# A Mamba scan moved to (channel, state) partitions: one-hot products on TensorE, the C product on GpSimd, convolution and projections folded into TensorE

## The chip, the cores and the metric

One core of one Trainium2 chip. The metric is the device time of one execution in microseconds (us). Fast executions of one kernel agree within 1% here (the widest apart are 10080.98 and 10161.75 us), and only executions of the fast state are compared. A ratio is the mean time of one kernel's fast runs over the mean time of the fast runs of the kernel before in the same rounds, so it is not quite the ratio of the medians that are quoted.

## The reference, cut to what matters

A non-local attention, a convolution block with a Mamba layer ("layer 1"), a bidirectional Mamba along both image axes ("layer 2", four more sets of weights), and a dynamic filter. The part that changes is the Mamba layer, which runs five times:

```
xz = einsum('blc,dc->bld', h, in_proj_w);  xm, z = split(xz, 2)
xc = silu(conv1d(xm, convd_w, causal, depthwise, 4 taps) + convd_b)
dt, B, C = split(einsum('bld,ed->ble', xc, x_proj_w), [4, 16, 16])
dt = softplus(einsum('blr,dr->bld', dt, dt_proj_w) + dt_proj_b)
step:  h = exp(dt*A) * h + dt*B*xc;   y = einsum('bds,bs->bd', h, C)     # 128 channels d, 16 states s
y = (y + xc*Dp) * silu(z);  return einsum('bld,cd->blc', y, out_proj_w)
```

All data are float32.

## The kernel before

128 channels lie on the partitions. A unit of the scan is 768 tokens of one batch and direction; it takes sixteen steps, one for each state. B and C of a state are one value a token, and TensorE copies them to all partitions with a broadcast product; the sum over states is an identity product that accumulates in PSUM.

```
for s in range(D_STATE):                              # one step = one state, 128 channels x 768 tokens
    nc.scalar.activation(da, u.dt, AF.Exp, scale=w.A[:, s : s + 1])
    ...                                               # zero da where a sequence starts
    if last is not None: add(*last)                   # y += identity x hc: two products
    cs = self.broadcast(w.C[s], u.xc)                 # two products of 384 columns
    nc.vector.tensor_mul(two(bx), two(u.u), bs)       # u * B
    if s + 1 < D_STATE: bs = self.broadcast(w.B[s + 1], u.xc)      # two products
    nc.vector.tensor_tensor_scan(h, da, bx, init, ALU.mult, ALU.add)
    nc.vector.tensor_mul(two(hc), two(h), cs)         # h * C
    next(other, None)                                 # a piece of the next unit's head
```

The head of the next unit (projection, convolution with four VectorE instructions, gate, step width dt by softplus, u = dt * xc) is a generator of which one piece is taken a step.

Of the kernel before, what the change touches and what calls it, by code (L numbers as in the profile page):

```python
# [26 lines left out]
P = 128  # L27
# [41 lines left out]
def rows_of(b):  # L69
    return slice(b * C, (b + 1) * C)  # L70

# [344 lines left out]
def mamba_weights(k, pool, i):  # L416

    nc = k.nc
    a = pool.tile([P, D_STATE], FP, name=f"A{i}")
    nc.scalar.activation(a, k.col(f"A_log{i}"), AF.Exp)  # L420
    nc.vector.tensor_scalar_mul(a, a, -1.0)
    in_w = k.mat(f"in_w{i}")
    if i:
        nc.vector.tensor_scalar_mul(in_w, in_w, k.col(f"norm_w{i}"))
    x_w = k.mat(f"x_w{i}")
    return SimpleNamespace(
        A=a,
        in_w=in_w,
        dt_x=x_w[:, :DT_RANK],
        B=[x_w[:, DT_RANK + s : DT_RANK + s + 1].to_broadcast([P, P]) for s in range(D_STATE)],  # L430
        C=[x_w[:, DT_RANK + D_STATE + s : DT_RANK + D_STATE + s + 1].to_broadcast([P, P]) for s in range(D_STATE)],
        dt_w=k.dtw[:, bass.ts(i, P)],
        conv_w=k.col(f"convd_w{i}"),
        conv_b=k.col(f"convd_b{i}"),
        dt_b=k.col(f"dt_b{i}"),
        Dp=k.col(f"Dp{i}"),
        out_w=k.mat(f"out_w{i}"),
    )


class Mamba:
# [8 lines left out]
    def __init__(self, k, wk, ps_bc, ps_y, ps_m):  # L450
        self.k, self.nc = k, k.nc
        self.wk, self.ps_bc, self.ps_y, self.ps_m = wk, ps_bc, ps_y, ps_m

    def mm(self, lhsT, rhs, m=P):
        p = self.ps_m.tile([P, NB], FP, tag="m", name="mm")
        self.nc.tensor.matmul(p[:m, :HALF], lhsT=lhsT, rhs=rhs, start=True, stop=True)  # L456
        return p[:m, :HALF]

    def work(self, tag, **kw):
        return self.wk.tile([P, CH], FP, tag=tag, name=tag, **kw)  # L460

    def head(self, u):
# [3 lines left out]
        tokens = [self.k.xb[rows, u.c0 + j * HALF : u.c0 + (j + 1) * HALF] for j in range(2)]  # L466
        pad = D_CONV - 1

        n, t = (1, CH) if u.carry else (SEQS, W)
        xp = self.wk.tile([P, n * (t + pad)], FP, tag="xp", name="xp")  # L470
        xp3 = xp.rearrange("p (n t) -> p n t", n=n)
        at = 0 if u.rev else pad
        edge = xp3[:, :, t:] if u.rev else xp3[:, :, :pad]
        if u.carry:
            nc.gpsimd.tensor_copy(edge[:, 0, :], u.carry.hist)
        else:
            nc.gpsimd.memset(edge, 0.0)
        for j in range(2):
            p = self.mm(w.in_w[rows, :P], tokens[j])
            if u.carry:  # L480
                nc.scalar.copy(xp[:, at + j * HALF : at + (j + 1) * HALF], p)
            else:
                m = SEQS // 2
                nc.scalar.copy(xp3[:, j * m : (j + 1) * m, at : at + W], p.rearrange("p (n t) -> p n t", n=m))  # L484
        if u.carry:
            nc.gpsimd.tensor_copy(u.carry.hist, xp[:, CH:])
        yield

        acc = self.work("acc", bufs=1)
        acc3 = acc.rearrange("p (n t) -> p n t", n=n)  # L490
        for j in range(D_CONV):
            by = j if u.rev else pad - j
            tap = w.conv_w[:, pad - j : pad - j + 1]
            if j == 0:
                nc.vector.tensor_scalar(acc3, xp3[:, :, by : by + t], tap, w.conv_b, ALU.mult, ALU.add)
            else:
                nc.vector.scalar_tensor_tensor(acc3, xp3[:, :, by : by + t], tap, acc3, ALU.mult, ALU.add)  # L497
                yield

        u.xc, u.gate = self.work("xc"), self.work("gate")  # L500
        pz = [self.mm(w.in_w[rows, P:], tokens[j]) for j in range(2)]
        nc.scalar.activation(u.xc, acc, AF.Silu)
        for j in range(2):
            nc.scalar.activation(u.gate[:, halves[j]], pz[j], AF.Silu)  # L504
# [4 lines left out]
        low = self.wk.tile([DT_RANK, CH], FP, tag="low", name="low", bufs=1)  # L509
        for j in range(2):  # L510
            nc.scalar.copy(low[:, halves[j]], self.mm(w.dt_x, u.xc[:, halves[j]], DT_RANK))
        yield
        e, u.dt = self.work("e", bufs=1), self.work("dt")
        for j in range(2):
            p = self.mm(w.dt_w, low[:, halves[j]])
            nc.scalar.activation(e[:, halves[j]], p, AF.Abs, bias=w.dt_b)
            nc.scalar.activation(u.dt[:, halves[j]], p, AF.Relu, bias=w.dt_b)
        yield
# [3 lines left out]
        yield  # L522
# [3 lines left out]
        nc.gpsimd.tensor_add(log, log, e)  # L526
        nc.gpsimd.tensor_add(u.dt, u.dt, log)
        yield
        u.u = self.work("u")
        nc.gpsimd.tensor_mul(u.u, u.dt, u.xc)  # L530

    def broadcast(self, lhsT, xc):

        p = self.ps_bc.tile([P, 2, NB], FP, tag="bc", name="bc")
        for j in range(2):
            self.nc.tensor.matmul(p[:, j, :HALF], lhsT=lhsT, rhs=xc[:, bass.ts(j, HALF)], start=True, stop=True)  # L536
        return p[:, :, :HALF]

    def scan(self, u, other):
        nc, w = self.nc, u.w  # L540
        y = self.ps_y.tile([P, 2, NB], FP, tag="y", name="y_ssm")

        def two(t):
            return t.rearrange("p (j n) -> p j n", j=2)

        def add(s, hc):
            for j in range(2):
                nc.tensor.matmul(  # L548
                    y[:, j, :HALF], lhsT=self.k.ident, rhs=hc[:, bass.ts(j, HALF)], start=s == 0, stop=s == D_STATE - 1
                )  # L550

        bs = self.broadcast(w.B[0], u.xc)
        last = None
        for s in range(D_STATE):
            da = self.work("da", bufs=3)
            nc.scalar.activation(da, u.dt, AF.Exp, scale=w.A[:, s : s + 1])  # L556
            if not u.carry:

                first = W - 1 if u.rev else 0
                nc.gpsimd.memset(da.rearrange("p (n t) -> p n t", n=SEQS)[:, :, first : first + 1], 0.0)  # L560
            if last is not None:
                add(*last)
            cs = self.broadcast(w.C[s], u.xc)
            bx = self.work("bx")
            nc.vector.tensor_mul(two(bx), two(u.u), bs)  # L565
            if s + 1 < D_STATE:
                bs = self.broadcast(w.B[s + 1], u.xc)
            h = self.work("h")
            step = slice(None, None, -1) if u.rev else slice(None)
            init = u.carry.state[:, s : s + 1] if u.carry else 0.0  # L570
            nc.vector.tensor_tensor_scan(h[:, step], da[:, step], bx[:, step], init, ALU.mult, ALU.add)  # L571
            if u.carry:
                nc.gpsimd.tensor_copy(u.carry.state[:, s : s + 1], h[:, CH - 1 :])
            hc = self.work("hc", bufs=3)
            nc.vector.tensor_mul(two(hc), two(h), cs)  # L575
            last = s, hc
            next(other, None)
        add(*last)
        yv = self.work("yv", bufs=1)
        nc.vector.scalar_tensor_tensor(two(yv), two(u.xc), w.Dp, y[:, :, :HALF], ALU.mult, ALU.add)  # L580
        u.y = self.work("yg", bufs=3)
        nc.gpsimd.tensor_mul(u.y, yv, u.gate)

    def run(self, units):

        for _ in self.head(units[0]):
            pass
        for i, u in enumerate(units):
            before = units[i - 1].tail(units[i - 1]) if i else ()
            after = self.head(units[i + 1]) if i + 1 < len(units) else ()  # L590
            other = chain(before, after)
            self.scan(u, other)
            for _ in other:
                pass
        for _ in units[-1].tail(units[-1]):
            pass


def mamba_pools(tc):
# [3 lines left out]
        tc.tile_pool(name="ssm_bc", bufs=2, space=PSUM),  # L603
        tc.tile_pool(name="ssm_y", bufs=1, space=PSUM),
        tc.tile_pool(name="ssm_m", bufs=2, space=PSUM),
# [3 lines left out]
def layer1(k):  # L609
# [41 lines left out]
    with ExitStack() as pools:  # L651
        ws, *rest = [pools.enter_context(p) for p in mamba_pools(tc)]
        m = Mamba(k, *rest)
        w = mamba_weights(k, ws, 0)
        carries = []
        for b in range(B):
            hist = ws.tile([P, D_CONV - 1], FP, name=f"hist{b}")
            state = ws.tile([P, D_STATE], FP, name=f"state{b}")
            nc.gpsimd.memset(hist, 0.0)
            nc.gpsimd.memset(state, 0.0)  # L660
            carries.append(SimpleNamespace(hist=hist, state=state))
# [25 lines left out]
def bi_mamba(k, which, along_h, lin_w, lin_b):  # L687
# [27 lines left out]
    with ExitStack() as pools:  # L715
        ws, *rest = [pools.enter_context(p) for p in mamba_pools(tc)]
        m = Mamba(k, *rest)
        w = [mamba_weights(k, ws, i) for i in which]
# [4 lines left out]
        def tail(u):  # L723
            rows = rows_of(u.b)
            n = HALF // W
            for j in range(2):
                s0 = u.c0 // W + j * n
                x = xs[rows, s0 : s0 + n, :]
                p = m.ps_m.tile([P, NB], FP, tag="m", name="po_bi")
                for d, one in enumerate((u.forward, u)):  # L730
                    at = rows_of(d)
                    nc.tensor.matmul(  # L732
                        p[at, :HALF], lhsT=w[d].out_w, rhs=one.y[:, bass.ts(j, HALF)], start=True, stop=False
                    )
                    nc.tensor.matmul(  # L735
# [160 lines left out]
```

## Time and profile before

| what | before |
|---|---|
| time | 12640.72 us (12632.42 to 12644.66) |
| scan stages, 120 units | 9350 us, 78 us a unit |
| all else (attention, norms, filter) | 3284 us |
| TensorE busy | 94% |
| VectorE busy | 79% |
| GpSimd busy | 14% |
| granted TensorE clock, mean | 0.977 |

TensorE is the bound and two engines have room. The lines that show it are in the prediction; read the busy shares first, then the wait behind each VectorE group: VectorE waits for broadcast products (953 us in all), TensorE waits for little (29 us before its broadcast products, 319 before its identity products).

### The profile page before, as it was taken

What the parts mean: (1) busy time and instruction counts of PE and PEld (TensorE: products, weight loads), DVE (VectorE), ACT (ScalarE), POOL (GpSimd) and SP (SyncE); (2) the same over time, 40 slices, a digit from 0 to 9 for tenths busy, and PEclk for the clock granted to TensorE, in tenths of its full rate; (3) what the DMA queues carried; (4) which work ended last, traced back from release to release, by engine and by line L of the source; (5) the groups of instructions that cost most, each with busy time, mean ns of one, the idle gap of its engine ahead of it and who ended that gap; (6) DMA issues with size and microseconds to landing.
All of it is one profiled execution on the core that took longest, in us unless ns stands there. A gap on an engine that the chain in (4) does not pass through costs nothing. (4 is left out here: it accounts for less than half of the span.)

```text
span 12634.1 us, 96887 instructions
## 1 busy us (share of the span) xinstructions
PE 11881.0 (94%) x37382; PEld 5579.8 (44%) x37382; DVE 10031.1 (79%) x7909; ACT 4985.3 (39%) x5408; POOL 1789.1 (14%) x2732
## 2 busy tenths in 40 slices
PE   9999999987999998999999999998999999999996
PEld 3333333323444443444444444443444444444443
DVE  4666566667888888888888888887888888888888
ACT  3444344444333333333333333333333333333332
POOL 0000000002222221111111111110111111111110
PEclk9999899998999998999999999998999999999998
DMA  0000000000000000000000000000000000000000
GB/s 20 1 1 1 1 1 1 1 1 0 0 0 0 0 0 0 0 0 1 0 0 0 0 0 1 0 0 0 0 0 1 0 0 0 0 0 0 0 0 15
DMA packets 2206, 17.03 MB, mean 1 GB/s; under 512 B 196, under 2 KB 324, under 8 KB 1096
## 3 DMA queue, kind: packets, MB, share of 16 engines
q1 hardware_dynamic: 1440, 9.44, 0.2%
q8 instruction: 294, 4.82, 0.2%
q14 instruction: 176, 1.44, 0.0%
q10 hardware_dynamic: 296, 1.33, 0.0%
HBM read 6.05 MB, written 4.72 MB: 1 GB/s over the span
## 5 line engine op out<-in xcount | busy, mean ns | idle before, releaser
L536 PE MATMUL bc<-xc,mats 128*128 128x384 f32 x15360 | 5282.9, 487 | 29.2 <-DVE bx L565 29.2
L536 PEld LDWEIGHTS bc<-xc,mats 128*128 128x128 f32 x15360 | 2924.9, 190 | 2077.4 <-DVE bx L565 34.4
L556 ACT ACTIVATE da<-dt,A 128x768 f32<-128x768 f32 x1920 | 1798.1, 937 | 4300.6 <-DVE h L571 4029.6
L548 PE MATMUL y_ssm<-hc,ident 128*128 128x384 f32 x7680 | 2963.8, 509 | 319.2 <-DVE hc L575 296.6
L571 DVE TENSOR_TENSOR_SCAN h<-da,bx 128x768 f32<-128x768 f32 x1536 | 2939.5, 1914 | 143.3 <-DVE bx L565 3.2
L575 DVE TENSOR_TENSOR hc<-h,bc 128x768 f32<-128x768 f32 x1920 | 1831.3, 954 | 752.3 <-PE bc L536 639.0
L548 PEld LDWEIGHTS y_ssm<-hc,ident 128*128 128x128 f32 x7680 | 1304.3, 189 | 1902.7 <-DVE hc L575 990.4
L565 DVE TENSOR_TENSOR bx<-u,bc 128x768 f32<-128x768 f32 x1920 | 1828.6, 952 | 326.6 <-PE bc L536 314.3
L267 DVE TENSOR_TENSOR acc_e<-acc_e,e 128x1536 f32<-128x1536 f32 x792 | 1390.3, 1755 | 763.2 <-ACT e L211 724.5
L211 ACT ACTIVATE e<-f_exp 128x1536 f32<-128x1536 f32 x864 | 1207.2, 1449 | 1218.9 <-PE f_exp L201 1218.9
L218 PE MATMUL y_att<-e,xb 128*64 128x512 f32 x5184 | 1242.5, 601 | 0.0
L201 PE MATMUL f_exp<-theta,phi 64*128 64x512 f32 x5184 | 1236.4, 608 | 0.4 <-ACT e L211 0.4
L560 POOL MEMSET da<- 128x8 f32 x1536 | 166.2, 113 | 5575.7 <-ACT da L556 5575.7
L201 PEld LDWEIGHTS f_exp<-theta,phi 64*128 64x128 f32 x5184 | 469.1, 187 | 757.0 <-issue 463.7
L571 DVE TENSOR_TENSOR_SCAN h<-da,state,bx 128x768 f32<-128x768 f32 x384 | 763.7, 1989 | 42.1 <-DVE bx L565 0.5
L218 PEld LDWEIGHTS y_att<-e,xb 128*64 128x64 f32 x5184 | 341.3, 136 | 830.7 <-issue 830.1
L556 ACT ACT_TABLE_LOAD x351 | 450.3, 1283 | 65.6 <-DVE h L571 60.6
L456 PE MATMUL mm<-xb,mats 64*128 64x384 f32 x960 | 422.9, 534 | 38.5 <-ACT xp L484 15.4
L240 POOL TENSOR_TENSOR xa<-xa,t_att 64x512 f32<-64x512 f32 x36 | 45.4, 1261 | 2721.6 <-ACT t_att L238 2721.6
L525 POOL TENSOR_TENSOR e<-e,kept 128x768 f32<-128x768 f32 x120 | 360.9, 3008 | 313.8 <-ACT log L521 313.8
L497 DVE SCALAR_TENSOR_TENSOR acc<-xp,cols,acc 128x768 f32<-128x768 f32 x360 | 374.1, 1039 | 7.4
L504 ACT ACT_TABLE_LOAD x234 | 300.2, 1283 | 151.8 <-PE mm L456 148.9
(124 smaller groups left out, 5499.1 us busy)
## 6 DMA issues: line engine op xcount, KB each, us to landing
xa<-in_x SPq DMA_DIRECT2D x6, 768.0 KB, 10.0
out<-xb SPq DMA_DIRECT2D x4, 1152.0 KB, 4.4
mats<-in_mats ACTq DMA_DIRECT2D x1, 1218.0 KB, 7.6
cols<-in_cols ACTq DMA_DIRECT2D x1, 71.5 KB, 9.3
dtw<-in_dtw ACTq DMA_DIRECT2D x1, 10.0 KB
```

What stands on the lines that cost most here:

```text
L201: nc.tensor.matmul(fs[j // 3][:, bass.ts(j % 3, NB)], lhsT=phi[at, bass.ts(m // 2, P)], rhs=theta[at, bass.ts(i, NB)], start=True, stop=True,)
L211: nc.scalar.activation(e, f, AF.Exp)
L218: nc.tensor.matmul(y[rows_of(m % 2)], lhsT=g[:, m, :], rhs=es[j // 3][:, bass.ts(j % 3, NB)], start=m < 2, stop=m >= KEYS - 2,)
L267: nc.vector.tensor_add(acc, acc, e)
L456: self.nc.tensor.matmul(p[:m, :HALF], lhsT=lhsT, rhs=rhs, start=True, stop=True)
L497: nc.vector.scalar_tensor_tensor(acc3, xp3[:, :, by : by + t], tap, acc3, ALU.mult, ALU.add)
L536: self.nc.tensor.matmul(p[:, j, :HALF], lhsT=lhsT, rhs=xc[:, bass.ts(j, HALF)], start=True, stop=True)
L548: nc.tensor.matmul(y[:, j, :HALF], lhsT=self.k.ident, rhs=hc[:, bass.ts(j, HALF)], start=s == 0, stop=s == D_STATE - 1)
L556: nc.scalar.activation(da, u.dt, AF.Exp, scale=w.A[:, s : s + 1])
L565: nc.vector.tensor_mul(two(bx), two(u.u), bs)
L571: nc.vector.tensor_tensor_scan(h[:, step], da[:, step], bx[:, step], init, ALU.mult, ALU.add)
L575: nc.vector.tensor_mul(two(hc), two(h), cs)
```

## The change

The intent is to take the scan off TensorE's bound. A step now holds eight channels times sixteen states on the 128 partitions, so B and C lie once per unit in a (channel, state) layout and need no broadcast a step. Instead u and dt are spread from 8 partitions to 128 by one-hot products that contract over 32 rows only (A is folded into the one for dt), and the sum over states is a one-hot product with 32 output rows ("gather"). Four such products are meant to run at once on the four strips of the array. VectorE multiplies by B in place in PSUM, GpSimd takes the product with C, the convolution becomes four accumulating products with the taps folded into the weights, and the low-rank step and dt projection become one matrix. The core of the diff, cut:

```
-            cs = self.broadcast(w.C[s], u.xc)
-            nc.vector.tensor_mul(two(bx), two(u.u), bs)
-            nc.vector.tensor_tensor_scan(h[:, step], da[:, step], bx[:, step], init, ALU.mult, ALU.add)
-            nc.vector.tensor_mul(two(hc), two(h), cs)
+    def spread(self, now, later):            # u of the next step, dt of the one after
+        for j in range(2):
+            for what, at in ((0, now), (1, later)):
+                ...
+                self.nc.tensor.matmul(self.side(...), lhsT=(self.t.spread if what == 0 else u.w.decay)[rows, q],
+                    rhs=(u.u if what == 0 else u.dt)[rows, cols], start=True, stop=True)
+        self.nc.scalar.activation(da, u.pda[step][:, NB - HALF : NB + HALF], AF.Exp)
+    def scan(self, u, step):
+        bx, da = u.pu[step][:, NB - HALF : NB + HALF], u.da[step]        # bx stays in PSUM
+        nc.vector.tensor_mul(two(bx), two(bx), each(u.B))
+        nc.vector.tensor_tensor_scan(h[:, way], da[:, way], bx[:, way], 0.0, ALU.mult, ALU.add)
+        nc.gpsimd.tensor_mul(two(hc), two(h), each(u.C))
+    def gather(self, u, step):               # two steps at once, four products on column strips
+        for s in (step - 1, step):
+            for j, r in enumerate(self.groups(s)[2]):
+                nc.tensor.matmul(u.py[32 * r : 32 * r + 32, :HALF], lhsT=self.t.gather[:, q], rhs=u.hc[s][...], ...)
...                                           # in run(), for step s of unit i, n steps in all:
+            if s == 4:                        # from here one piece of the next head a step, then the last tail
+                other = chain(after, before)
+            if s == self.STEPS - 2:           # what is left of it
+                for _ in other: pass
+            self.spread(at(n + 1), at(n + 2))
+            self.scan(u, s)
+            if s % 2 == 0 and n >= 2: self.gather(*steps[n - 1])
+            next(other, None)
```

## The prediction

> **What bounds the kernel now.** I read the engine totals and the slices first, then the costliest groups, then windows over the stages, then the timeline of one unit of the scan (one unit is 768 tokens of one batch and direction; 24 units in layer 1, 48 in each half of layer 2, 120 in all).
>
> ```profile
> PE 11881.0 (94%) x37382; PEld 5579.8 (44%) x37382; DVE 10031.1 (79%) x7909; ACT 4985.3 (39%) x5408; POOL 1789.1 (14%) x2732
> PE   9999999987999998999999999998999999999996
> DVE  4666566667888888888888888887888888888888
> PEclk9999899998999998999999999998999999999998
> ```
>
> TensorE is full in every slice. The first eight slices are the attention; the scan fills the rest, and there VectorE is already at 80%. [...]
>
> ```profile
> 100.00:2760.00 2660.00, 2607.01 (x10894) 889.57 (x10890) 1669.46 (x1043) 1244.64 (x916) 44.14 (x35) 0.99 0.00 1
> 2950.00:4800.00 1850.00, 1722.62 (x5048) 900.74 (x5048) 1612.58 (x1335) 696.82 (x815) 403.13 (x544) 1.00 0.00 0
> 4910.00:8690.00 3780.00, 3651.67 (x10420) 1835.82 (x10420) 3176.44 (x2632) 1431.02 (x1701) 649.99 (x1051) 1.00 0.00 0
> 8790.00:12510.00 3720.00, 3589.01 (x10421) 1832.59 (x10420) 3163.94 (x2632) 1437.42 (x1709) 652.63 (x1052) 1.00 0.00 0
> 8700.00:8770.00 70.00, 41.80 (x52) 13.37 (x52) 66.48 (x47) 25.41 (x49) 0.00 (x0) 0.50 0.00 0
> ```
>
> Columns: length, then busy us and count of PE, PEld, DVE, ACT, POOL, then the clock. Rows two to four are the scans: 1850 + 3780 + 3720 = 9350 us, 78 us a unit. The other 12634 - 9350 = 3284 us (attention, norms, filter) are not touched. The last row is a norm stage: TensorE 60% busy, clock 0.50.
>
> ```profile
> L536 PE MATMUL bc<-xc,mats 128*128 128x384 f32 x15360 | 5282.9, 487 | 29.2 <-DVE bx L565 29.2
> L571 DVE TENSOR_TENSOR_SCAN h<-da,bx 128x768 f32<-128x768 f32 x1536 | 2939.5, 1914 | 143.3 <-DVE bx L565 3.2
> L575 DVE TENSOR_TENSOR hc<-h,bc 128x768 f32<-128x768 f32 x1920 | 1831.3, 954 | 752.3 <-PE bc L536 639.0
> L565 DVE TENSOR_TENSOR bx<-u,bc 128x768 f32<-128x768 f32 x1920 | 1828.6, 952 | 326.6 <-PE bc L536 314.3
> ```
>
> Each of 1920 steps takes four broadcast products and two identity products on TensorE; VectorE waits 953 us for them.
>
> ```profile
> 7022.56 1.76 DVE L571 TENSOR_TENSOR_SCAN h<-da,bx 128x768 f32<-128x768 f32 x1
> 7022.57 3.36 POOL L525 TENSOR_TENSOR e<-e,kept 128x768 f32<-128x768 f32 x1 [2.07 <-ACT log L521]
> 7022.61 2.74 PE L536 MATMUL bc<-xc,mats 128*128 128x384 f32 x8
> 7024.42 0.95 DVE L575 TENSOR_TENSOR hc<-h,bc 128x768 f32<-128x768 f32 x1
> ...
> 7026.01 1.80 POOL L526 TENSOR_TENSOR log<-log,e 128x768 f32<-128x768 f32 x1
> 7026.45 2.98 DVE L571 TENSOR_TENSOR_SCAN h<-da,bx 128x768 f32<-128x768 f32 x1
> ...
> 7043.73 1.82 POOL L582 TENSOR_TENSOR yg<-yv,gate 128x768 f32<-128x768 f32 x1
> ...
> 7044.33 0.95 DVE L565 TENSOR_TENSOR bx<-u,bc 128x768 f32<-128x768 f32 x1
> ```
>
> Three readings. A 384-column product costs 2.74 / 8 = 0.34 us. A scan whose two inputs lie in SBUF excludes GpSimd: 1.76 alone, 2.98 when GpSimd came first, and GpSimd 1.80 becomes 3.36 behind a scan. A VectorE product with one input in PSUM does not: bx 0.95 and yg 1.82 lie over each other unharmed.
>
> [...] The attention agrees for pairs: its half-array products of 512 columns come every 2607 / 10894 = 0.24 us against 0.46 scaled from 0.34; quads are not in this trace. [...]
>
> **The change part by part.** The state and channel go on the partitions, eight channels a step; a step still has 128 x 768 elements.
> - TensorE: per step, four spread products on four row strips (u of the next step, dt of the one after), per two steps four gather products on four column strips. Six products at 0.34 become about 1.5 product times, if quads overlap: about 0.4 + 0.4 us of stream, perhaps 0.75 for a spread if its four weight loads (0.19 each) go one by one. Convolution adds 8 products a unit; the low-rank step and the copies to a 4-row tile go. Per unit 16 x 0.75 + 8 x 0.6 + 18 x 0.34 = 23 us, far below 78.
> - VectorE: loses hc (1920 x 0.95) and the convolution (0.69 + 3 x 1.04 a unit). Per step bx 0.95 + wait for its own result 0.11 + scan 1.76 + 0.05 = 2.87, not stretched by GpSimd, since bx is now in PSUM. Unit of layer 2: 16 x 2.87 = 45.9, two half yv 1.2, kept 0.56, residual 0.8 on average: 48.4 us. Layer 1 splits each scan: two of 384 at 0.8 + 0.22 (the carried scan's 1.82 less 1.6) = 2.04, so 3.15 a step, 50.4 + 2.9 = 53.3 a unit.
> - GpSimd: hc 16 x 1.82, four head products 7.3, two half yg 2: 38 us a unit. Enough as a mean, not at the seam.
> - ScalarE: 16 x 0.94, copies 8 x 0.48, four of 0.58, Exp and Ln 1.7, one Silu of 1536 about 1.5, two table loads 2.6: 27 us. Not a bound; table loads fall from over five to two a unit.
>
> Floor: 24 x 53.3 + 96 x 48.4 = 5926, so 9210 + some 60 for building tables and folded weights: 9270 us.
>
> **The seam of a unit, by the order of the built program.** After scan 11 GpSimd has, back to back, hc 11, three head products, hc 12, u and the memset of dt: 6 x 1.88 + 0.1 = 11.4 us[...]. On TensorE the next unit's first dt product, which needs that memset, stands between the two halves of the spread of u for step 15. VectorE gets to step 15 after 0.56 + 3 x 2.87 = 9.2 us; the second half lands at about 12.8 to 13.3. Stall: about 4 us in each of 96 units (layer 1 has no memset and takes dt some 4 us earlier: about 1). In every second unit the second residual product waits for the first residual addition, and the next unit's spread waits behind it: 1.8 us at full clock, 4 at half. The long Silu entry delays exp by about 4 us, within the two steps of lead.
>
> **Clock.** [...] At half clock the convolution (4 x 0.69 = 2.8 us) between a gather that waits for hc and the next spread costs about 2.8 us a unit, and the seam about 2 more. Full clock: 48.4 + 4 + 0.9 + 0.3 = 53.6 a unit; half clock about 58.5. I take 56.5, and 57 for layer 1: 96 x 56.5 + 24 x 57 = 6790. Sum 3284 + 60 + 6790 = 10134, said as 10100 us.
>
> **The rivals.**
> - GpSimd and VectorE exclude each other after all [...]. For: 2.98 and 3.36 above. Against: the bx and yg lines[...]. Then a step is 0.95 + about 3.2, a unit 70 us, the time about 11700.
> - Quads do not overlap. A unit has 96 products at 0.34 plus 18: 39 us at full clock, so VectorE stays the bound, but with less slack; if the clock were at half too, 78 us a unit and no gain. Against: the pairs of the attention. About 10700 for a mix.
> - VectorE runs at its floor, since the waits hide: 9270 to 9500. Against: the order of TensorE and GpSimd at the seam.
> - Writing bx into PSUM is dearer than into SBUF: each 0.1 us costs 1920 x 0.1 = 190 us.
>
> **Range and chances.** 10100 us; 9600 to 10700 eight times in ten: below lies full clock with hidden seams, above weak overlap or a dear bx. Even the port rival is over 7% faster. Faster 0.98, same 0.01, slower 0.01.
>
> **What would show it.** Right: VectorE over 80% busy in the scans and the largest; scans at a median of 1.76 with GpSimd beside them; hc at 1.8 on GpSimd; a wait of 3 to 5 us before one bx a unit on the spread of step 15; the four spread products within 1 us at full clock; a clock of 0.5 to 0.8 in the scans. Wrong: scans near 3 us (port); TensorE over 85% busy (no overlap); no long bx wait and a time under 9500; a clock of 1.0 and a time near 9700.

## The result, and the profile after

The changed kernel takes **10703.12 us** (10690.35 to 10731.61, four runs), against 12636.65 for the kernel before on the same chip: ratio 0.8472, 95% interval 0.8453 to 0.8492. The record of this result has no word on correctness; every experiment built on it is marked correct, but that holds even for the two from which convolution taps were taken, so the mark does not cover the taps. So it is faster, as predicted, but 600 us slower than the predicted 10100 and just above the upper end of the range (10700).

The page of the changed kernel, engine totals and slices:

```profile
PE 9253.1 (86%) x38998; PEld 3067.6 (29%) x38998; DVE 7512.1 (70%) x6112; ACT 4326.3 (40%) x5082; POOL 4687.8 (44%) x3186
PE   9999999999688888688888888888788888888884
PEclk9999989999778888778888888888688888888886
```

TensorE is still the busiest engine, and VectorE, meant to be the bound, is busy for 70%. The clock is lower in the scan, slices 11 on. Two windows inside layer 2's scans and one of 14 us inside a unit (length, then busy us and count of PE, PEld, DVE, ACT, POOL, then clock):

```profile
4579.00:7510.00 2931.00, 2544.24 (x10890) 812.61 (x10886) 2130.33 (x1705) 1161.17 (x1559) 1799.76 (x1087) 0.82 0.00 1
7677.00:10595.00 2918.00, 2480.76 (x10990) 809.63 (x10986) 2137.33 (x1725) 1166.72 (x1566) 1817.32 (x1098) 0.85 0.00 1
7022.00:7036.00 14.00, 12.19 (x38) 3.71 (x38) 8.44 (x7) 7.34 (x10) 8.20 (x5) 0.63 0.01 1
```

A unit takes about 61 us (the last scan's 2918 / 48 = 60.8), against 78 before. TensorE is busy for 85 to 87% of it, but at a clock of 0.82 to 0.85, and lower in some stretches (0.63 in the 14 us). The costliest groups (instructions counted after x, then busy us and mean ns of one, then us of idle time before them and what ended most of it):

```profile
L649 POOL TENSOR_TENSOR hc<-h,C 128x768 f32<-128x768 f32 x1920 | 3470.2, 1809 | 1882.6 <-DVE h L647 1481.4
L647 DVE TENSOR_TENSOR_SCAN h<-da,u_s 128x768 f32<-128x768 f32 x1536 | 2693.5, 1754 | 202.9 <-DVE u_s L637 5.4
L637 DVE TENSOR_TENSOR u_s<-u_s,B 128x768 f32<-128x768 f32 x1920 | 1828.6, 952 | 907.4 <-PE dt_s L617 561.0
...
L572 DVE TENSOR_SCALAR kept<-e 128x768 f32<-128x768 f32 x120 | 67.7, 564 | 632.7 <-ACT e L567 632.7
```

The scan is 1.754 us with GpSimd running beside it, and GpSimd's C product 1.81: no stretching on either side, where the kernel before had 1.914 on average for the scan. The B product into PSUM costs 0.952, what it cost into SBUF before. All of the loss is in waits. VectorE's waits in the scan stages, by what it waited for (us in total, times, longest; e and kept are steps of the softplus that makes dt, u_s and dt_s are u and dt after the spread, lin is the residual product):

```profile
DVE kept L572 <- ACT e L567: 601.8, 118, 25.8
DVE u_s L637 <- PE dt_s L617: 558.9, 446, 6.3
DVE u_s L637 <- PE u_s L617: 326.5, 169, 11.1
DVE xa L863 <- PE lin L862: 214.0, 77, 6.1
```

These sum to 1701 us, 14.2 us a unit. The first line stands for ScalarE, but the timeline of one unit shows what ScalarE waited for:

```profile
7024.77 1.00 PE L617 MATMUL u_s<-u,spread 32*128 32x384 f32 x2 [1.81 <-DVE h L647]
...
7025.71 1.65 PE L513 MATMUL mm<-raw,step 128*128 128x384 f32 x2
...
7027.28 1.64 PE L617 MATMUL u_s<-u,spread 32*128 32x384 f32 x2
...
7030.28 1.65 PE L617 MATMUL dt_s<-dt,decay 32*128 32x384 f32 x4
7031.86 1.50 PE L660 MATMUL y_ssm<-hc,gather 128*32 128x384 f32 x6
...
7033.29 1.65 PE L513 MATMUL mm<-raw,step 128*128 128x384 f32 x2
...
7035.92 0.84 ACT L567 ACTIVATE e<-e 128x768 f32<-128x768 f32 x1
...
7036.79 0.56 DVE L572 TENSOR_SCALAR kept<-e 128x768 f32<-128x768 f32 x1 [4.98 <-ACT e L567]
...
7047.05 0.91 PE L617 MATMUL dt_s<-dt,decay 32*128 32x384 f32 x2 [1.21 <-POOL dt L587]
...
7049.84 0.97 DVE L637 TENSOR_TENSOR u_s<-u_s,B 128x768 f32<-128x768 f32 x1 [3.61 <-PE dt_s L617]
```

Read it in order. TensorE runs with no pause from 7024.77 to 7035 at about half clock (0.53 granted): two step products of the next unit's head at 1.65 us each, one spread in three pieces, one gather in two. "x2" on the step product is one product in two records: every float32 product of this kernel has two (15360 records of broadcast before for 1920 x 4 = 7680 products). The second step product is the last in that stretch, Exp follows it, and "kept", which VectorE's order has ahead of the next B product, waits 4.98 us. Ten microseconds of TensorE stand against about 5.5 of VectorE's two steps. The last two lines are the seam that the prediction described: the first dt product of the new unit waits for the memset of dt, and the B product of step 15 waits 3.61 us. Over the 96 units of layer 2 the wait there is 3.59 us on average.

At full clock a 384-column product is not 0.34 us either. The changed kernel's timeline and its clock around one convolution half (four products, eight records):

```profile
6019.99 2.80 PE L536 MATMUL conv<-xb,taps 64*128 64x384 f32 x8
```

```profile
6020.00:6024.00 4.00, 4.00 (x19) 2.01 (x18) 2.85 (x3) 0.84 (x2) 2.98 (x2) 1.00 0.00 0
```

2.80 / 4 = 0.70 us a product at a clock of 1.00. The prediction had that as its half-clock figure.

### The profile page after: what moved, and what is told of

It reads as the page before. It is cut to its first block, busy times and chain, and to the rows that moved or that the text cites. A ratio compares the mean times of both kernels' runs of the same rounds, so it can differ in the third digit from the quotient of the medians.

```text
span 10712.3 us, 100413 instructions
## 1 busy us (share of the span) xinstructions
PE 9253.1 (86%) x38998; PEld 3067.6 (29%) x38998; DVE 7512.1 (70%) x6112; ACT 4326.3 (40%) x5082; POOL 4687.8 (44%) x3186
## 4 chain that ended last, share of the span: by engine, by line
PE 38%; DVE 21%; POOL 8%; ACT 5%; issue 2%; DVEq 0%; POOLq 0%; ACTq 0%
DVE h L647 10%; PE u_s L617 9%; PE y_ssm L660 7%; PE mm L513 7%; DVE u_s L637 6%; PE conv L536 5%; PE dt_s L617 5%; POOL hc L649 3%; DVE h L643 3%; PE lin L858 2%; PE conv L530 1%; ACT da L628 1%; POOL e L573 1%; POOL log L579 1%; POOL dt L579 1%
## 5 line engine op out<-in xcount | busy, mean ns | idle before, releaser
L649 POOL TENSOR_TENSOR hc<-h,C 128x768 f32<-128x768 f32 x1920 | 3470.2, 1809 | 1882.6 <-DVE h L647 1481.4
L617 PE MATMUL u_s<-u,spread 32*128 32x384 f32 x7680 | 2331.3, 607 | 730.0 <-DVE h L647 556.0
L647 DVE TENSOR_TENSOR_SCAN h<-da,u_s 128x768 f32<-128x768 f32 x1536 | 2693.5, 1754 | 202.9 <-DVE u_s L637 5.4
L628 ACT ACTIVATE da<-dt_s 128x768 f32<-128x768 f32 x1920 | 1553.7, 809 | 2652.2 <-PE dt_s L617 2646.4
L637 DVE TENSOR_TENSOR u_s<-u_s,B 128x768 f32<-128x768 f32 x1920 | 1828.6, 952 | 907.4 <-PE dt_s L617 561.0
L617 PE MATMUL dt_s<-dt,decay 32*128 32x384 f32 x7680 | 2219.9, 626 | 283.2 <-ACT da L628 187.1
L660 PE MATMUL y_ssm<-hc,gather 128*32 128x384 f32 x7680 | 1534.2, 616 | 52.7 <-POOL hc L649 52.0
L617 PEld LDWEIGHTS u_s<-u,spread 32*128 32x128 f32 x7680 | 819.2, 213 | 2214.0 <-DVE h L647 1149.1
L617 PEld LDWEIGHTS dt_s<-dt,decay 32*128 32x128 f32 x7680 | 716.5, 214 | 730.9 <-ACT da L628 338.5
L643 DVE TENSOR_TENSOR_SCAN h<-da,state,u_s 128x384 f32<-128x384 f32 x768 | 738.8, 1001 | 48.6 <-DVE u_s L637 1.5
```

The lines of the kernel that those rows point to most:

```text
L617: self.nc.tensor.matmul(self.side((u.pu if what == 0 else u.pda)[step], j), lhsT=(self.t.spread if what == 0 else u.w.decay)[rows, q], rhs ...
L628: self.nc.scalar.activation(da, u.pda[step][:, NB - HALF : NB + HALF], AF.Exp)
L637: nc.vector.tensor_mul(two(bx), two(bx), each(u.B))
L647: nc.vector.tensor_tensor_scan(h[:, way], da[:, way], bx[:, way], 0.0, ALU.mult, ALU.add)
L649: nc.gpsimd.tensor_mul(two(hc), two(h), each(u.C))
L660: nc.tensor.matmul(u.py[32 * r : 32 * r + 32, :HALF], lhsT=self.t.gather[:, q], rhs=u.hc[s][:, j * HALF : (j + 1) * HALF], start=q == 0, s ...
```

## The experiments

Seventeen kernels ran. In the expectations, L says that the next unit's head comes too late, T that TensorE's capacity binds, C that the granted clock does, and G that a gather which waits for its C product holds up TensorE's queue. "Port" is the prediction's and the expectations' name for the theory that the scan or the B product and GpSimd exclude each other. Where the expectations speak of passes, the two records of a product in the trace are meant. Unless stated otherwise the edit is made on the changed kernel, and its median of fast runs is to be compared with 10703.

### What the parts of the change are worth

**B product back into SBUF.**

```
-        nc.vector.tensor_mul(two(bx), two(bx), each(u.B))
+        bxs = self.work("bxs");  nc.vector.tensor_mul(two(bxs), two(bx), each(u.B));  bx = bxs
```

> The changed kernel with the result of bx written to a tile in SBUF instead of in place in PSUM, so that the scan has two SBUF inputs while GpSimd makes hc. Port theory (two SBUF inputs and GpSimd exclude each other): scan and hc take turns, 1.75 + 1.8 = 3.6 us a step or more, scans over 2.5 us on average, unit at least 16 x 3.7 + 6 = 65 us, time 11200 to 12400. If the place of bx does not matter: within 1% of 10703, scans at 1.75.

Measured: 12543.75 us, ratio 0.9924: nearly the whole gain is gone, a little more than the port theory's range allowed. The scan's group in this kernel:

```profile
L649 DVE TENSOR_TENSOR_SCAN h<-da,bxs 128x768 f32<-128x768 f32 x1536 | 3528.3, 2297 | 203.7 <-DVE bxs L638 6.8
```

The mean scan went from 1754 to 2297 ns, with the same arithmetic. One scan at 6999.17 took 3.19 us, and what GpSimd does besides the C product took 1987 us in place of 1218 (5473.0 - 3486.1 and 4687.8 - 3470.2). With the B product in PSUM the two engines work at once at 1.754 and 1.81 us, with both inputs of the scan in SBUF the scan is stretched; the placement is worth 12544 - 10703 = 1840 us, of which 3528.3 - 2693.5 = 835 us are longer scans of layer 2; the rest was not taken apart, and the granted clock fell to 0.77.

**C product back on VectorE.**

```
-        nc.gpsimd.tensor_mul(two(hc), two(h), each(u.C))
+        nc.vector.tensor_mul(two(hc), two(h), each(u.C))
```

> The C product back on VectorE, all else as in the changed kernel (one part of the change undone). VectorE gets 16 x 0.95 = 15 us a unit and GpSimd loses 29 us, so the waits for GpSimd at the seam (3.6 us) go. If VectorE bounds the unit: 61 + 15 - 4 = 72 us, about 11900 us. If TensorE and its clock bound it (theories T, C), part of the 15 us hides in VectorE's idle time (13 us a unit): 10800 to 11300.

Measured: 11715.69 us, ratio 0.9269, between the two ranges. GpSimd's share is worth 1010 us, 8.4 us a unit, of the 15 us a unit that VectorE is spared: VectorE's waits fell by much of the rest at the same time, from 1701 to 1044 us (kept 452, u_s 339 and 89, the residual 165).

**Convolution back on VectorE** (the four tap instructions of the kernel before, with the padded copy).

> The convolution back on VectorE (one part of the change undone): TensorE loses six products of two passes, 6 x 0.69 = 4.1 us a unit, VectorE gets 0.69 + 3 x 1.04 = 3.8 us, up to 3 us more where it meets GpSimd. Theory T: as TensorE loses 4 us a unit, 10300 to 10500. Theory L: the 1.4 to 1.7 us that the convolution holds up bx go, 3.8 to 6 us come: 10900 to 11200. Theory C: the clock falls below 0.84 in the scans as well, so rather the upper end of that.

Measured: 10910.16 us, ratio 0.8632, inside L's range. The folded convolution is worth 207 us, 1.7 us a unit.

### When the head of the next unit starts

**Head from step 1 on.**

```
-            if s == 4:
+            if s == 1:
```

> The changed kernel with one number changed: the next unit's head starts at step 1 of a unit, not at step 4. Theory L (lead): the head's chain (convolution, Silu, step product, Exp, three GpSimd products) comes too late at the seam, because every product is two passes and costs 0.69 us, not 0.34. Then the wait of the dt product for GpSimd's memset (3.6 us before one bx in each unit of layer 2) goes, the wait of kept (5 us in a unit) stays since kept moves along with the head: about 10703 - 96 x 3.6 = 10350 us. Theory T (throughput): TensorE, 86% busy in the scans at a clock of 0.84, is the bound itself; a wait that goes comes back elsewhere: within 1% of 10703.

Measured: 10180.56 us, ratio 0.8052 (0.8028 to 0.8075). A gain of 523 us, more than L asked for. VectorE's wait on "kept", which L had expected to stay, fell from 602 to 52 us, all of it at the two starts of scans. A new wait came up, in TensorE's queue:

```profile
PE y_ssm L660 <- POOL dt L587: 395.5, 92, 4.8
PE u_s L617 <- DVE h L647: 337.9, 383, 1.8
PE y_ssm L660 <- POOL hc L649: 156.6, 302, 3.4
```

In the changed kernel the gather (y_ssm) waited 48 us for hc in the scans; here GpSimd runs e, log, dt and u of the head nearly in a row, the C products come behind them, and the gather waits 552 us in all.

**The same, with "kept" one step later.**

```
+        yield
         kept = self.work("kept", bufs=1)
```

> As e1, and the VectorE product kept (with the GpSimd subtraction behind it) is placed one step later, so that VectorE does not reach it before ScalarE has made e. Theory L: the 5 us of kept in each unit go as well: 10350 - 120 x 5 = 9750 us, and the wait before kept falls from 633 us to under 150. Theory T: within 1.5% of 10703, with the lost waits found again before bx.

Measured: 10259.23 us, ratio 0.8114. A miss: slower than without by 0.8%. The wait it was to remove was gone already; that GpSimd's later chain is what costs is likely, not shown.

**Order of the four spread products** (head at step 4 again): both of u, then both of dt.

```
-        for j in range(2):
-            for what, at in ((0, now), (1, later)):
+        for what, at in ((0, now), (1, later)):
+            for j in range(2):
```

> The changed kernel with the order of the four spread products changed: both halves of u first, then both halves of dt (before: u, dt, u, dt). In this order no half of u stands behind a dt product that waits for GpSimd or ScalarE. Theory L: the 3.6 us before step 15 go in layer 2, and some of the 561 us that bx waits for a dt product: 10300 to 10450 us. Theory T: within 1% of 10703.

Measured: 10692.28 us, ratio 0.8456, no change, as T expected. This run is instructive all the same. The wait on "kept" fell from 602 to 52 us as in the early head, but the B product's wait for the spread rose from 885 to 1258 (dt_s and u_s labels together) and that of the residual from 214 to 373. The name of a wait moved and the time did not: I read it as the same stretch of TensorE, under whichever label VectorE meets it.

### GpSimd's order, and the gather's place in TensorE's queue

**Early head, GpSimd's order pinned**, with one product of the head between C products at a time, and u and dt's memset correspondingly later.

```
+        self.k.tc.keep_in_program_order(...)        # around hc, yg, e, log, dt, u and the memset
-                if lhsT is w.bc[0]: ... tensor_add(log), tensor_add(dt) in the pieces of B
+                if lhsT is w.bc[0] and j: ... log;  elif lhsT is w.bc[1] and j: ... dt;  then u
```

> The early head with GpSimd's own order pinned: its products of the head (e, log, dt, u) stand one at a time between the C products, not three and four in a row as in e1. In e1 VectorE waited 776 us for bx on the spread and 180 us on h's buffers, mostly at the seam, where the C products were late. If GpSimd's order makes that wait (L, GpSimd's part), 9750 to 9950. If TensorE at a low granted clock makes it (C), within 1.5% of 10181.

Measured: 10222.17 us, ratio 0.8087: a miss for L, no gain over 10181, and within the 1.5% that C gave. In a stretch of 2800 us of layer 2, TensorE's wait at the gather fell from 242 to 158 us, and the first dt product waited 110 us for dt's memset, which now came later.

**The same, with the residual products at steps 5 and 8 and a fourth h buffer.**

```
+            if s in (5, 8): next(before, None)       # the last unit's tail, apart from the head
-        h = self.work("h", bufs=3)
+        h = self.work("h", bufs=4)
```

> As e10, with the residual products of the last unit moved from the end of the unit to steps 5 and 8, where the head has no product of its own, and four buffers for h in place of three. L: lin's wait (135 us in e1) goes and no product crowds the seam: 50 to 200 us below e10, the sum of all early and spread-out work then 9550 to 9850. C: within 1% of e10.

Measured: 10402.32 us, ratio 0.8242: slower than the run before by 1.8%, a miss for L and C alike. The two parts of this edit were not taken apart.

**Gathers two steps later**, with the head at step 4.

```
-            if s % 2 == 0 and n >= 2: self.gather(*steps[n - 1])
+            if s % 2 == 0 and n >= 4: self.gather(*steps[n - 3])       # and seven hc buffers, not five
```

> The changed kernel with only its gathers two steps later (the C products then have two steps more; seven hc buffers in place of five). TensorE waited for hc only 12 us in 2800 in the changed kernel, so the theory that a gather holds the queue (G) expects no gain here: within 1.5% of 10703. A gain of over 3% would mean that the gather holds the spread even where the profile puts the wait elsewhere.

Measured: 10797.06 us, ratio 0.8543: 0.9% slower, as G expects where the gather hardly waits.

**Gathers two steps later and the head at step 1** (and three buffers for the convolution and gate).

> The early head of e1 with the gathers two steps later (and three buffers for the convolution and gate, which live longer). G: in e1 TensorE waited 242 us in 2800 for y_ssm's operand, at the seam, and the next spread stood behind it in the queue; these waits go: 9700 to 9950. If it is the granted clock or TensorE's own work that holds the seam, within 1.5% of 10181.

Measured: **9800.91 us**, ratio 0.7754 (0.7734 to 0.7774), inside G's range. The gather's wait is gone (2.2 us are left of 552) and TensorE waits, if at all, for VectorE:

```profile
PE u_s L617 <- DVE h L647: 572.4, 579, 3.0
PE u_s L617 <- DVE h L643: 131.4, 137, 2.2
...
PE y_ssm L660 <- POOL hc L649: 2.2, 3, 1.3
```

Late gathers cost 0.9% with the late head and gained 3.7% with the early one, here together with the third buffer. The reading is an in-order queue: a gather at its head that waits for GpSimd holds the next spread. In the early-head trace TensorE sat idle before a gather 92 times, 4.3 us on average, until GpSimd's memset of dt was done (the 395.5 us above); one such memset ends at 7022.92, and the B product that needs the next spread starts at 7028.83. The third buffer is a rival that no run has alone: with two, ScalarE waited 395 us for GpSimd's yg before it wrote the next unit's convolution, and with three most of its idle time there ends with the convolution's product instead (532 of 712 us). What speaks for the queue is the place of the gain: before the fifth B product after "kept" VectorE sat idle for 4.18 and 3.40 us, waiting for the spread, in two units of the early head (7028.83 and 7087.75), and for 0 and 0.63 us in two units here (6052.05 and 6111.23; in the second, 3.87 us for a residual product come before it). VectorE's six largest waits in the scan stages fell from 1220 to 851 us.

**The same on the pinned kernel.**

> The same on e10 (early head, GpSimd's products of the head one at a time). G: e10's waits for hc, 158 us in 2800, go, and what is left is dt's memset (110): 9750 to 10000. Clock or work: within 1.5% of 10222.

Measured: 10132.47 us, ratio 0.8009: only 0.9% better than without, a miss for G and within the 1.5% of the other theory. In those 2800 us the gather's wait is gone, but TensorE waits 187 us for dt's memset, which the pinned order had put later. Pinning did not help.

### TensorE's own work, and its clock

**One tap of the convolution in place of four** (a wrong result on purpose): six products a unit less.

```
-        for j in range(D_CONV):
+        for j in range(1):
...                                                  # stop flag at j == 0
```

> The changed kernel with one tap of the convolution in place of four (a wrong result on purpose): six products of 384 columns fewer a unit, by the measured 0.69 us each 4.1 us of TensorE a unit at full clock, 8.3 at half; by the 0.34 of the prediction 2.0. If TensorE's own time at the seam sets the unit there, the time falls by 120 x 2 to 120 x 8: 9750 to 10460, and by more than 120 x 2.1 = 250 only if a product costs 0.69. If the lead alone sets it (the taps lie in steps 5 and 6, where VectorE has work), within 1.5% of 10703.

Measured: 10332.81 us, ratio 0.8168. 370 us less, 3.1 us a unit for six products, 0.51 each, inside the range for TensorE's own time at the seam. At full clock 0.34 a product could not give that much, but at half clock it could (0.68), so this run alone does not tell the two costs apart; the row above at a clock of 1.00 does. The record marks this run and the next as correct, so its check does not notice the missing taps.

**The same on the early head with late gathers.**

> e13 with one tap of the convolution in place of four (a wrong result on purpose). In the changed kernel these six products a unit were worth 370 us (3.1 us a unit). If TensorE's time holds the unit with the early head too, 9400 to 9600; if the lead has taken it off the path, within 1.5% of 9801.

Measured: 9584.92 us, ratio 0.7581. 216 us, 1.8 us a unit, inside the first range: TensorE's time is still on the path, though less of it.

**The two u products of each spread made twice.**

```
+            for j in range(2):     # the same product once more into the same place
+                self.nc.tensor.matmul(self.side(u.pu[step], j), lhsT=self.t.spread[rows, q], rhs=u.u[rows, cols], ...)
```

> The changed kernel with the two spread products of u made twice (same operands, same result): 16 x 2 more row-strip products in a unit, a pair of two passes of 0.42 us, so 16 x 0.84 = 13 us of TensorE a unit. If the throttled clock is what costs (theory C), the fuller TensorE holds a clock near 1.0 and the time stays within 2% or falls. If TensorE's own work is what costs (theory T), it rises by most of 120 x 13 = 1600 us, to about 12000. Theory L: TensorE has some slack outside the seam, so 11100 to 11700.

Measured: 10493.34 us, ratio 0.8299: more work, and 2% *faster*, as C allowed. The mean clock rose from 0.859 to 0.917, and the wait on "kept" fell from 602 to 149 us.

**The two dt products made twice instead.**

> The changed kernel with the two spread products of dt (not of u) made twice, behind the four: the same 13 us of extra TensorE work a unit as in e4, but no bx waits for it. Theory C (the granted clock): the clock rises to about 0.92 as in e4, the wait of kept falls, and as nothing is put before bx the time is below e4: 10300 to 10480 us. Theory T (TensorE's own work): above 10703. If e4 was an accident of the order: 10700.

Measured: one fast run of 10893.99 us and one slow one of 11141.10, so no ratio. The clock of the fast run was 0.89. Inconclusive: in this place the repeated products stand in front of the next u product, and VectorE waited 1236 us for that one.

**u products twice, early head.**

> The head of the next unit at step 1 (as in e1) and the two u products of the spread made twice (as in e4). It asks what made e4 faster. If it was the granted clock alone (C), it adds to the early head, whose clock was 0.89: 10181 - 210 = 9970, clock 0.93 or more. If e4 was faster because its head chain came in time (kept's wait fell there from 602 to 149 us, which the early head has removed already), nothing is left to win: 10130 to 10300. If TensorE's capacity binds (T), 13 us a unit more of it give over 10700.

Measured: 10586.58 us, ratio 0.8373, clock 0.922. 4% slower than the early head alone; all three expectations missed. TensorE's wait for hc had grown to 686 us, so the gather held the queue for longer; why it waited longer was not taken apart.

**u products twice, early head and late gathers.**

> The fastest kernel so far (e13: early head, gathers two steps later, 9801 us, clock 0.86) with the two u products of each spread made twice, 13 us more of TensorE work a unit by the measured pace. If the clock that was granted is what is left (C), the clock goes to 0.92 or more and the time falls below 9650. If TensorE's own work is (T), it rises to 10000 or more. Within 1.5% of 9801: the two cancel.

Measured: **9748.51 us**, ratio 0.7708 (0.7695 to 0.7721), clock 0.953; 0.5% faster than without the copies, so the two cancel. Windows over the same stretch of layer 2's first scan, first of the early head with late gathers, then with the doubled products:

```profile
4600.00:6900.00 2300.00, 2021.06 (x9878) 692.69 (x9878) 1919.15 (x1547) 1056.44 (x1417) 1633.50 (x988) 0.83 0.00 1
```

```profile
4600.00:6900.00 2300.00, 2128.68 (x12764) 861.15 (x12764) 1927.47 (x1563) 1068.76 (x1439) 1655.40 (x997) 0.99 0.00 1
```

In the same 2300 us TensorE did 29% more records and VectorE 1% more instructions: the higher clock went with the copies and about paid for them. It is the fastest kernel of the study that leaves no work out, but its extra products compute nothing new; without them the kernel is as good to within half a per cent. The clock was 0.83 with TensorE idle for 279 of the 2300 us, and 0.99 with 171 us idle. TensorE's waits for the scans of layer 2 were 1.0 us on average and 3.0 at the longest in the first kernel, 0.54 and 1.5 in the second. Long waits are not needed for a low clock: in 5900 to 6900 of the changed kernel no wait of TensorE was longer than 2.4 us, and the granted clock was 0.83 all the same, with slices of four microseconds down to 0.50 (5916 to 5920, TensorE busy throughout). What sets the clock was not shown.

## Why the prediction was wrong, by its own steps

**What held.** The argument about the place of bx held in both directions (scan 1.754 us and C product 1.81 with bx in PSUM, scan 2.297 with both inputs in SBUF). Writing into PSUM was not dearer (0.952 us in both kernels). All outside the scans, tables included, came out at 3376 us (the span of 10712 less 7337 from the first to the last scan of each stage; 3321 by the same measure before), for a predicted 3284 + 60. Four products on four strips do overlap: a spread of four took 0.93 us (7000.35 to 7001.28 in the changed kernel, at a clock of 1.00), against 2.80 for the four of a convolution half, one behind the other:

```profile
7000.35 0.59 PE L617 MATMUL u_s<-u,spread 32*128 32x384 f32 x2 [1.81 <-DVE h L647]
7000.36 0.59 PE L617 MATMUL dt_s<-dt,decay 32*128 32x384 f32 x2
...
7000.77 0.49 PE L617 MATMUL u_s<-u,spread 32*128 32x384 f32 x2
7000.79 0.49 PE L617 MATMUL dt_s<-dt,decay 32*128 32x384 f32 x2
```

The seam on dt's memset was there, 3.59 us on average for a predicted 4. The two steps of lead before exp were enough for VectorE: the scans of layer 2 waited for exp 0.5 us in all, though dt products on TensorE waited 186 us for it. And the floor of VectorE was a little lower than predicted: a step is 2.74 us and not 2.87, since the next B product starts before the scan's record ends; 16 x 0.13 = 2.1 us a unit in the prediction's favour.

**What failed.** The step "A 384-column product costs 2.74 / 8 = 0.34 us", and what was built on it: "Per unit 16 x 0.75 + 8 x 0.6 + 18 x 0.34 = 23 us, far below 78". With TensorE's work put so low, the path at the seam had no wait before "kept": "VectorE gets to step 15 after 0.56 + 3 x 2.87 = 9.2 us" counts kept with its 0.56 us alone, and it waited 5 us for e in nearly every unit (602 us, 118 times).

The eight records at 7022.61 were four products, not eight. A product costs 0.70 us at full clock in a row of them, and 1.65 for one by itself at about half clock (0.53 granted). The prediction's own window row had the contradiction in it: 10420 records over 48 units are 217 records or 108.5 products a unit; at 0.34 each they would have been 37 us of TensorE, and the row has 3651.67 / 48 = 76.1; 108.5 x 0.70 = 76.0. (The comparison of pairs in the attention, 0.24 us against 0.46, survives, since both of its sides were counted in records.)

With the right cost the terms of a unit are 16 x 0.85 for the spreads (start to start at full clock, 7000.35 to 7001.20), 8 x 0.78 for gathers whose operands are there (6027.17 to 6027.95), and 19 x 0.70 for the rest (eight of the convolution, eight of the head, three residual ones on average): 33 us, an estimate from these rows. The prediction's last term, 18 x 0.34, was off by two; its spreads and gathers were low by 12 and 23%. The trace has more still: 2480.76 / 48 = 51.7 us busy a unit at a mean clock of 0.85, some 44 at full clock by an estimate from these two, since these rows are best cases and a spread or gather in pieces, as in the timeline above, takes longer. Even 33 us at full clock are 66 at half, more than a unit of VectorE, if the time of a product at least doubles there, as 0.70 and 1.65 us say. So TensorE was not far from a bound but had no room whenever the clock fell, and the clock fell to 0.82.

The prediction allowed about 8 us of stalls a unit over the floor (56.5 - 48.4). VectorE's waits were 14.2. The six in excess, less the two that the floor was too high, are the four to five by which the unit was off: about 61 against 57, and 120 x 4.5 = 540 of the 600 us.

The prediction's signs can be read now. VectorE was to be over 80% busy in the scans and the largest; it was 73% busy (2130 of 2931 us), below TensorE. TensorE over 85% busy was to mean that nothing overlaps; it was 85 to 87% busy although quads overlap, since a product costs double. The clock was to be 0.5 to 0.8, an estimate: the trace before had 0.50 in a norm stage with TensorE 60% busy, but also from 1400 to 1450 us with TensorE busy throughout. It was 0.82 to 0.85.

**What the runs show of it, and what they don't.** That the lead was too short is shown: three steps more of it gained 523 us. That a product costs more than 0.34 is shown by the row at a clock of 1.00; that TensorE's own products are on the path is shown by the six that were left out, worth 0.51 each. That the wait lies in "kept" itself is refuted, although the profile puts 602 us there: changing the order of the spread took that wait away and left the total at 10692 against 10703. That the last 3.7% over the early head were held by the gather's place in the queue is what the runs with late gathers and the place of the lost wait say; the third buffer that came with them was not tried alone. That it was the half clock which made the stretch before "kept" ten microseconds long is read from the timeline and not isolated. And the gain from doubled products on the changed kernel is not split between the clock and the shift in order that comes with it; where nothing held the queue, the higher clock only about paid for the added work. With the early head and late gathers a unit still takes about 6435 / 120 = 53.6 us (the span of 9811 less the 3376 that the changed kernel spends outside its scans), against a floor of 48.4 - 2.1 = 46.3; the 1.8 us that six convolution products are worth there say that TensorE has a part in the difference, and the rest is open.

## What to carry to other kernels

Before a duration from a row goes into a sum, check the sum against a total that is known: records divided by the number of products in the program, and product cost times their number against the busy time of the unit before. Where an instruction waits for a slow producer, look at what stands behind it on its engine, and try it later: with an early head, two steps and the buffers for them (two of hc, one of raw) were worth 3.7%, and where the gather hardly waited the two steps cost 0.9%. And don't take the label of a wait for its cause: change what it waits for, and see whether the total moves or only the label.
